# A gated graph layer followed by a normalised one: where the checks on newly loaded matrix rows stand at a change of batches

## The chip, the cores and the metric

The kernel runs on one core of one Trainium2 chip. The metric is the device time of one launch in microseconds (us). A core has five engines that run at the same time and each work through their own instructions in order: TensorE (PE in the profile; its weight loads are PEld), VectorE (DVE), ScalarE (ACT), GpSimd (POOL) and SyncE (SP), which here issues most of the transfers (DMAs) between the memory outside the core and its SBUF. TensorE writes into banks of PSUM, which VectorE and ScalarE read.

## What is computed

Sixteen graphs (batches) of 1024 nodes with 128 channels each go through two layers. `adj` holds a 1024x1024 matrix of zeros and ones for each batch.

```python
def gru_cell(m, h, w_ih, w_hh, b_ih, b_hh):
    xr, xz, xn = split(m @ w_ih.T + b_ih, 3)
    hr, hz, hn = split(h @ w_hh.T + b_hh, 3)
    r, z = sigmoid(xr + hr), sigmoid(xz + hz)
    n = tanh(xn + r * hn)
    return (1 - z) * n + z * h

# layer 0
h = maximum(layernorm(x), 0)
for i in range(4):
    m = einsum('bjn,bjd->bnd', adj, h @ weight[i])
    h = gru_cell(m, h, w_ih[i], w_hh[i], b_ih[i], b_hh[i])
x = x + h * nodemask
# layer 1
h = maximum(layernorm(x), 0)
for i in range(4):
    h = relu(einsum('bnm,bmc->bnc', adj, h @ W[i]) + b[i])
    h = gamma[i] * (h - mean(h)) * rsqrt(var(h) + eps) + beta[i]     # over batches and nodes
x = x + h
```

## The kernel before

The function `exact_path` computes both layers in a form that is exact only if the matrix entries can be held exactly in a shorter number format. Whether they can is read from their low 16 bits: every row tile of `adj` (128 rows by 1024 columns, float32) is looked through once, and the largest or summed low half goes into one column of the small tile `low`. If any is above zero, a general version runs afterwards. There are two ways to look through a row tile:

- `look` (line 606) is one VectorE reduction by maximum over the 1024 low halves (L610 in the profile);
- `glance` (line 580) is one ScalarE copy of the low halves with an accumulated sum (L586), for each row in its list. It writes its copy into a scratch tile called `junk`.

The first layer works on two streams of batches, A (`sa`: batches 0, 2, …) and B (`sb`: 1, 3, …). `half_step(one, two)` (line 1095) handles one iteration of each: stream `two` computes its gates, stream `one` its aggregation `adj.T @ h`. The calls alternate (`half_step(sa, sb)`, `half_step(sb, sa)`), each stream goes through four iterations for a batch (`self.i` from 0 to 3) and then takes the next one. The whole layer stands under a manual schedule: on every engine and queue the instructions run in the order in which the Python code emits them.

TensorE's part of a half step is `two.products(0)`, `two.products(1)` (the products for the gates, for columns 0 to 511 and 512 to 1023, called hf = 0 and 1) and then `one.agg_step(0)` and `one.agg_step(1)` (32 matmuls). Each gate has one PSUM bank, `g_r`, `g_z`, `g_hn`, `g_xn`, and both halves use the same four, so the products of hf = 1 can overwrite a bank only when what read it for hf = 0 is done. Around this, for each hf:

- `reset_gate`: sigmoid r on ScalarE (L1011), then two VectorE operations, L1012 (reads `g_hn`) and L1013 (reads `g_xn`);
- `candidate`: tanh on ScalarE (L1016);
- `less` (L1027 or L1029) and `mixed` (L1033, L1034) on VectorE; `update_gate`: sigmoid z on ScalarE (L1020, reads `g_z`);
- `high` (ScalarE) and `low` (VectorE, L942 or L926), for stream `one`: they split its features into two parts that the aggregation uses; `low(1)` is needed by `agg_step(1)`;
- at the end of `agg_step(1)`, two ScalarE copies of the result, `m` (L955), with which the next half step's products start.

Other work hangs on named places of a half step: `at(n, place, go)` (line 1059) enters a function for half step number n, and `due(place)` runs it. In order of emission the places are "ins", "start", "beside0", "mid", "beside1", "outs", "gap", "end". The norm of a batch to come is computed at "beside0" and "beside1", the sums of a finished batch at "gap".

The change of batches: when stream `two` is in its last iteration (`self.i == 3`) and has a batch to come, `fetch` (line 853) has SyncE load that batch's first four row tiles into four staging places (L572). Both streams use the same four places, A in one half step and B in the next. `first_four` (line 862) has GpSimd cast them into the row tiles that TensorE reads (L577). `last_four` (line 866), emitted behind z of hf = 1, emits four glances on ScalarE, one for each of rows 0 to 3, then the loads of rows 4 to 7 into the same four places, which must wait for the glances and casts of the rows before them, and their casts. Rows 4 to 7 are looked at in the following half step: for A by four looks at "start", so ahead of `reset_gate(0)` on VectorE, and for B by four glances at "gap". There are seven changes for each stream. In the half step after A's change comes B's, so B's first four loads wait for A's looks.

SyncE's queue in such a half step holds, in order: the incoming copies of a new batch's turned features ("ins", `pair_in`), the loads of rows 0 to 3, the outgoing copy of hf = 0, the loads of rows 4 to 7, the outgoing copies of hf = 1 and, at "end", of a turned input (`t_in`).

The second layer follows the first on the same core. It converts the stored matrix row by row and is not touched.

Of the kernel before, what the change touches and what calls it, by code (L numbers as in the profile page):

```python
# [341 lines left out]
def exact_path(  # L342
# [24 lines left out]
    NB = N // P  # L367
# [33 lines left out]
    def hw_tiles(b, name):  # L401
        return [keep.tile([P, N], F32R, tag=f"hw{b % 2}{s}", name=f"{name}_{s}") for s in range(2)]
# [130 lines left out]
    with ExitStack() as st:  # L533
# [36 lines left out]
        def stage_rows(b, stage, js):  # L570
            for j in js:
                nc.sync.dma_start(stage[j % 4], adj[b][j * P : (j + 1) * P, :])  # L572

        def round_rows(b, stage, js):
            ts = [gru_row(b, j) for j in js]
            for j, t in zip(js, ts):
                nc.gpsimd.tensor_copy(t, stage[j % 4])  # L577
            return ts

        def glance(b, stage, js):  # L580

            junk = work.tile([P, N], BF16, tag="junk", name=f"junk{b}_{js[0]}", bufs=1)
            for j in js:
                lows = stage[j % 4].bitcast(U16).rearrange("p (n t) -> p n t", t=2)[:, :, 0]
                k = b * NB + j
                nc.scalar.activation(junk, lows, AF.Copy, accum_out=low[:, k : k + 1])  # L586
# [19 lines left out]
        def look(b, row, j, part=0):  # L606

            lows = row.bitcast(U16).rearrange("p (n t) -> p n t", t=2)[:, :, 0]
            k = (b + part * B) * NB + j
            nc.vector.tensor_reduce(low[:, k : k + 1], lows, axis=AX.X, op=ALU.max)  # L610
# [7 lines left out]
        def transposes(batches):  # L618

            for b, rows in batches:  # L620
                adjT = turned_tile(f"adjT{b}")
                ahead = transpose_rows(b, rows[0], 0, adjT)
                for j in range(NB):
                    go = ahead
                    if j + 1 < NB:
                        ahead = transpose_rows(b, rows[j + 1], j + 1, adjT)
                    go()
                    yield j
                nc.gpsimd.dma_start(adjT_d[b].rearrange("k p n -> p k n"), adjT)
                yield NB  # L630
# [139 lines left out]
        class Stream:  # L770
# [95 lines left out]
            def last_four(self):  # L866
                if self.stage:
                    b, stage, self.stage = self.b + 2, self.stage, None
                    glance(b, stage, range(4))
                    stage_rows(b, stage, range(4, NB))  # L870
                    self.rows += round_rows(b, stage, range(4, NB))

                    def looks():
                        for j in range(4, NB):
                            look(b, stage[j % 4], j)

                    if self is sa:
                        at(clock[0] + 1, "start", looks)
                    else:
                        at(clock[0] + 1, "gap", lambda: glance(b, stage, range(4, NB)))  # L880

            def take(self):
                self.xt, self.y = self.next_x, self.next_y
# [173 lines left out]
        clock = [3]  # L1057

        def at(n, place, go):
            agenda.setdefault((n, place), []).append(go)  # L1060

        def due(place):
            for go in agenda.pop((clock[0], place), ()):
                go()
# [23 lines left out]
        def mids(two):  # L1088

            pace = small.tile([P, 1], F32, tag="pace", name=f"pace{clock[0]}")  # L1090
            nc.gpsimd.tensor_copy(pace, two.new[:, :1])
            feed.store()
            due("mid")

        def half_step(one, two, gated=None, halfway=None):

            feed.next_step()
            counts = (2, 1, 1)
            if one is sb and one.i == 0:
                feed.jobs = transposes([(s.b, s.rows) for s in (sa, sb)])  # L1100
                counts = (0, 0, 0)
            elif two is sb and two.i == 0:
                counts = (2, 2, 1)
            elif two is sa and two.i == 1 and two.across:
                counts = (3, 1, 1)
            due("ins")
            due("start")
            if one.i > 0:
                one.halves_back()
            else:  # L1110
                one.hw = hw_tiles(one.b, f"ghw{one.b}_0")
            two.fetch()
            feed.some(counts[0])
            two.products(0)
            two.reset_gate(0)
            due("beside0")
            two.candidate(0)
            two.less(0)
            one.high(0)
            two.update_gate(0)  # L1120
            one.low(0)
            two.mixed(0)
            two.half_away(0)
            two.first_four()
            if feed.full or (clock[0], "mid") in agenda:
                mids(two)
            one.high(1)
            feed.some(counts[1])
            two.products(1)
            two.reset_gate(1)  # L1130
            due("beside1")
            one.low(1)
            two.candidate(1)
            two.less(1)
            two.update_gate(1)
            two.last_four()
            two.mixed(1)
            two.half_away(1)
            due("outs")
            due("gap")  # L1140
            due("end")
            if gated:
                gated()
            one.agg_step(0)
            if halfway:
                halfway()
            feed.some(counts[2])
            one.agg_step(1)
            two.finish()
            clock[0] += 1  # L1150

        sa, sb = Stream(0), Stream(1)
        every = {getattr(mybir.EngineType, e) for e in ("PE", "DVE", "Activation", "Pool", "SP")}
        prep = st.enter_context(tc.tile_pool(name="prep", bufs=1))
        with tc.manual_schedule(engines=every):
# [20 lines left out]
            stage = keep.tile([P, NB, N], BF16, tag="adjT", name="stage", bufs=1).bitcast(F32)  # L1176
# [98 lines left out]
            first_step(sb, sa, lambda: turn_ih(prep, w_g, 2), lambda: ahead(2))  # L1275
            written[0] = False
            half_step(sa, sb, lambda: turn_ih(prep, w_g, 3), lambda: ahead(3))
            half_step(sb, sa)
            for s in range(3, B // 2 * L):
                half_step(sa, sb)  # L1280
                half_step(sb, sa)
# [301 lines left out]
```

## Time and profile before

| | |
|---|---|
| three runs | 1785.47, 1788.07, 1794.2 us; median 1788.07 |
| the profiled execution | 1789.26 us, its span 1787.5 |
| TensorE's granted clock | 0.999 |
| glances: count, one | 84; 1.06 us, and 0.19 for reading the sum |
| looks at staged rows: count, one | 36 (28 of them in the change of batches); 1.22 us |
| casts of staged rows on GpSimd: count, one | 112; 1.04 us median |
| loads of staged rows: count, size, issue to landing | 112; 512 KB; 3.5 / 5.7 / 7.9 us (least, median, most) |

All times of the profile belong to one execution. In a timeline a line has the start and the duration in us, the engine, the line of the kernel, what is done, and in brackets how long the engine had been idle and what ended it; merged instructions have a count. SPq is SyncE's queue: its lines are the issuing of transfers and not the transfers. A list of waits gives who waited for whom, the total in us, the number of times and the longest. A table of stretches gives the length, then each engine's busy time and number of instructions, TensorE's clock, and the share of time and the rate of the DMA engines.

### The profile page before, as it was taken

The page shows a single profiled execution, that of the slowest core. Times are in us where ns is not written, and L with a number is a line of the kernel's source. Part 1 is how long each engine was busy: PE and PEld are TensorE (multiplying, and loading weights), DVE is VectorE, ACT ScalarE, POOL GpSimd, SP SyncE. Part 2 cuts the span into 40 slices and gives each one's busy share as a digit, 9 for nine tenths or more (in the row PEclk, how much of TensorE's full clock was granted, in tenths as well). Part 3 has the DMA queues.
Part 4 walks back from the last instruction along what each step waited for, and adds up shares of the span by engine and source line. Part 5 has one row for each costly group of instructions (what it writes and reads, how often), then busy time and mean ns, then how long its engine had stood idle before and what let it go on. Part 6 is the DMA issues. An engine that isn't in the chain of part 4 may idle for free. (4 is left out here: it accounts for less than half of the span.)

```text
span 1787.5 us, 22335 instructions
## 1 busy us (share of the span) xinstructions
PE 1759.3 (98%) x6734; PEld 1191.7 (67%) x6734; DVE 1305.9 (73%) x2310; ACT 1107.6 (62%) x1713; POOL 379.3 (21%) x417
## 2 busy tenths in 40 slices
PE   9999999999999999999999999999999999999997
PEld 6565655565656565556555556577778888888886
DVE  7677877887887787887797787676666666666665
ACT  5356556556566556665655655476777767768765
POOL 4314323332331331422432333010100000000011
PEclk9999999999999999999999999999999999999999
DMA  7467657777676676776756768788766575767667
GB/s 259 135 175 262 189 163 272 179 208 241 204 200 213 223 212 197 245 202 202 260 169 186 265 174 227 256 287 311 271 228 241 207 253 201 245 224 245 238 217 268
DMA packets 363617, 400.16 MB, mean 224 GB/s; under 512 B 158188, under 2 KB 239888, under 8 KB 363488
## 3 DMA queue, kind: packets, MB, share of 16 engines
q1 hardware_dynamic: 342736, 323.59, 57.6%
q0 software_dynamic: 20224, 74.80, 11.3%
q8 instruction: 55, 0.90, 0.2%
q14 instruction: 74, 0.61, 0.1%
q10 hardware_dynamic: 528, 0.26, 0.0%
HBM read 267.47 MB, written 97.52 MB: 204 GB/s over the span
## 5 line engine op out<-in xcount | busy, mean ns | idle before, releaser
L524 PE MATMUL pm<-row,ghw 128*128 128x512 f32 x2048 | 503.6, 402 | 0.7 <-DVE ghw L926 0.6
L524 PEld LDWEIGHTS pm<-row,ghw 128*128 128x128 f32 x2048 | 383.8, 188 | 106.6 <-issue 29.2
L1016 ACT ACTIVATE r<-r,vecs 128x512 f32<-128x512 f32 x128 | 92.6, 723 | 255.0 <-DVE r L1013 253.1
L524 PE MATMUL pc_m<-wide,chw 128*128 128x512 f32 x1024 | 245.3, 395 | 0.0
L615 POOL CAST half<-row 128x1024 bf16<-128x1024 f32 x128 | 147.4, 1161 | 361.1 <-DMA adjT<-half 347.9
L524 PEld LDWEIGHTS pc_m<-wide,chw 128*128 128x128 f32 x1024 | 190.4, 188 | 41.9 <-issue 3.8
L524 PE MATMUL pc_g_r<-wide,chw 128*128 128x512 f32 x464 | 186.9, 403 | 0.3 <-ACT chw L501 0.3
L524 PE MATMUL pc_g_z<-wide,chw 128*128 128x512 f32 x464 | 181.0, 390 | 0.0
L577 POOL CAST row<-stage 128x1024 fp32r<-128x1024 f32 x112 | 128.6, 1156 | 243.7 <-DMA stage<-in_adj_dram 232.2
L1012 DVE SCALAR_TENSOR_TENSOR r<-g_hn,vecs,r 128x512 f32<-128x512 f32 x128 | 93.3, 729 | 117.9 <-ACT r L1011 66.9
L955 ACT COPY m<-pm 128x512 f32<-128x512 f32 x128 | 68.4, 585 | 163.5 <-PE pm L524 163.5
L1313 DVE CAST wide<-block 128x1024 fp32r<-128x1024 bf16 x160 | 109.9, 692 | 75.5 <-PE pc_m L524 48.3
L1313 DVE CAST wide<-packed 128x1024 fp32r<-128x1024 bf16 x160 | 110.1, 691 | 71.9 <-PE pc_g_z L524 53.5
L1311 ACT CAST wide<-packed 128x1024 fp32r<-128x1024 bf16 x96 | 100.6, 1048 | 58.5 <-PE pc_m L524 29.7
L993 PE MATMUL g_r<-m,w_mT 128*128 128x512 f32 x256 | 132.0, 597 | 3.4 <-ACT m L955 2.9
L1311 ACT CAST wide<-block 128x1024 fp32r<-128x1024 bf16 x96 | 100.7, 1049 | 53.9 <-PE pc_g_z L524 27.7
L993 PE MATMUL g_z<-m,w_mT 128*128 128x512 f32 x256 | 130.7, 592 | 0.0
L993 PE MATMUL g_xn<-m,w_mT 128*128 128x512 f32 x256 | 130.7, 592 | 0.0
L1361 DVE BATCH_NORM_STATS2 stats<-feat 128x6 f32<-128x512 f32 x128 | 84.1, 686 | 47.0 <-ACT feat L1360 45.9
L1029 DVE TENSOR_TENSOR h<-h,r 128x512 f32<-128x512 f32 x96 | 83.8, 872 | 41.9 <-ACT r L1016 41.8
L1033 DVE TENSOR_TENSOR h<-h,z 128x512 f32<-128x512 f32 x128 | 107.8, 842 | 6.8 <-ACT z L1020 0.2
L1011 ACT ACTIVATE r<-g_r,brz 128x512 f32<-128x512 f32 x128 | 87.9, 686 | 39.1 <-PE g_r L993 38.8
(186 smaller groups left out, 2830.5 us busy)
## 6 DMA issues: line engine op xcount, KB each, us to landing
block<-adjT_d SPq DMA_DIRECT2D x256, 256.0 KB, 4.7
packed<-adjT_d SPq DMA_DIRECT2D x256, 256.0 KB, 5.5
stage<-in_adj_dram SPq DMA_DIRECT2D x120, 512.0 KB, 5.7
adjT_d<-adjT POOLq DMA_DIRECT2D x16, 2048.0 KB, 7.7
cross_h<-t_h SPq DMA_DIRECT2D x92, 256.0 KB, 2.2
n_h<-cross_h SPq DMA_DIRECT2D x368, 64.0 KB, 2.0
xmid_d<-x POOLq DMA_DIRECT2D x16, 512.0 KB, 6.9
y<-ymid_d POOLq DMA_DIRECT2D x16, 512.0 KB, 5.4
```

The costliest lines, as they stand in the source:

```text
L524: nc.tensor.matmul(pm[hf], hw[s][:, j * P : (j + 1) * P], rows[j][:, hf * HALF : (hf + 1) * HALF], start=(j == 0 and s == 0), stop=(j == N ...
L577: nc.gpsimd.tensor_copy(t, stage[j % 4])
L615: nc.gpsimd.tensor_copy(t, row.bitcast(F32))
L993: nc.tensor.matmul(po, wT[:, i, g * C : (g + 1) * C], rhs, start=start, stop=stop)
L1011: nc.scalar.activation(r, pr, AF.Sigmoid, bias=brz[:, 3 * i : 3 * i + 1])
L1012: nc.vector.scalar_tensor_tensor(r, phn, b_hn(i), r, ALU.add, ALU.mult)
L1016: nc.scalar.activation(self.r, self.r, AF.Tanh, bias=b_in(self.i))
L1029: nc.vector.tensor_sub(ho, hin, self.r)
L1033: nc.vector.tensor_mul(ho, ho, self.z)
L1311: nc.scalar.copy(r, t)
L1313: nc.vector.tensor_copy(r, t)
L1361: nc.vector.bn_stats(stats[:, b * NH + hf, :], dst)
```

## The change

Only places in the order change. At both streams' changes the glances at rows 0 and 1 go ahead of `candidate(1)`, the tanh of hf = 1, behind sigmoid r (and behind what stands at "beside1"); those at rows 2 and 3 stay where they were, behind z. In the half step after A's change, the looks at rows 4 and 5 stay at "start" and those at rows 6 and 7 go to a new place "looks", behind `reset_gate(0)` and ahead of `less(0)` on VectorE. In the half step after B's, the glances at rows 4 and 5 go to "beside1", ahead of the tanh of hf = 1, and those at rows 6 and 7 stay at "gap".

```diff
             def last_four(self):
                 if self.stage:
                     b, stage, self.stage = self.b + 2, self.stage, None
-                    glance(b, stage, range(4))
+                    glance(b, stage, range(2, 4))
                     stage_rows(b, stage, range(4, NB))
                     self.rows += round_rows(b, stage, range(4, NB))
 
-                    def looks():
-                        for j in range(4, NB):
-                            look(b, stage[j % 4], j)
-
                     if self is sa:
-                        at(clock[0] + 1, "start", looks)
+                        for place, js in (("start", (4, 5)), ("looks", (6, 7))):
+                            at(clock[0] + 1, place, lambda js=js: [look(b, stage[j % 4], j) for j in js])
                     else:
-                        at(clock[0] + 1, "gap", lambda: glance(b, stage, range(4, NB)))
+                        for place, js in (("beside1", (4, 5)), ("gap", (6, 7))):
+                            at(clock[0] + 1, place, lambda js=js: glance(b, stage, js))
+
+            def first_glances(self):
+                if self.stage:
+                    glance(self.b + 2, self.stage, range(2))
...
             two.products(0)
             two.reset_gate(0)
             due("beside0")
+            due("looks")
             two.candidate(0)
             two.less(0)
             one.high(0)
...
             two.products(1)
             two.reset_gate(1)
             due("beside1")
+            two.first_glances()
             one.low(1)
             two.candidate(1)
             two.less(1)
```

## The prediction

> **What bounds the kernel now.** I read the page's first part first:
>
> ```profile
> PE 1759.3 (98%) x6734; PEld 1191.7 (67%) x6734; DVE 1305.9 (73%) x2310; ACT 1107.6 (62%) x1713; POOL 379.3 (21%) x417
> ```
>
> TensorE looks full, but matmul ends are modelled, so a short hold hides in it. I therefore took, from the timeline of TensorE, the start of the first hidden-state product (g_r<-h) of every half step of the first layer. They are numbered k = 0, 1, 2 … from 20.02 us. From k = 4 on, a half step takes 17.57 us unless it lies at a change of batches. Excess over 17.575 us:
>
> - k = 7, 15, 23, 31, 39, 47, 55 (stream B fetches): 1.49, 2.36, 2.09, 2.06, 0.75, 1.44, 2.38; sum 12.57
> - k = 8, 16 … 56: 0.30 to 0.37; sum 2.42
> - k = 9, 17 … 57: 0.01, 0.31, 0.11, 1.07, 0, 1.30, 1.03; sum 3.82
> - k = 34: 0.88; k = 6, 14 … 54 (stream A fetches) and all others: 0
>
> So the changes cost 19.7 us, 1.1% of the run; that is the most this change can win back. Stretches of k = 6, 7, 8:
>
> ```profile
> 133.38:150.96 17.58, 17.58 (x58) 10.57 (x57) 13.21 (x17) 14.92 (x28) 5.50 (x5) 1.00 0.61 207
> 150.96:170.03 19.07, 18.10 (x58) 10.38 (x56) 14.82 (x18) 9.91 (x17) 8.83 (x8) 1.00 0.85 296
> 170.03:187.91 17.88, 17.87 (x57) 10.49 (x56) 13.23 (x25) 10.98 (x21) 6.84 (x6) 1.00 0.67 197
> ```
>
> The second column is the length, then PE, PEld, DVE, ACT, POOL. No engine is full in k = 7; something is late. The timeline of k = 7 shows what:
>
> ```profile
> 146.75 3.87 SPq L572 DMA_DIRECT2D stage<-in_adj_dram  x4
> ...
> 150.33 1.22 DVE L610 TENSOR_REDUCE low<-stage 128x1 f32<-128x1024 uint16 x1
> ...
> 152.76 1.22 DVE L610 TENSOR_REDUCE low<-stage 128x1 f32<-128x1024 uint16 x1 [1.21 <-DMA stage<-in_adj_dram]
> ...
> 154.84 1.22 DVE L610 TENSOR_REDUCE low<-stage 128x1 f32<-128x1024 uint16 x1 [0.86 <-DMA stage<-in_adj_dram]
> ...
> 156.36 1.22 DVE L610 TENSOR_REDUCE low<-stage 128x1 f32<-128x1024 uint16 x1 [0.30 <-DMA stage<-in_adj_dram]
> 156.42 2.34 SPq L572 DMA_DIRECT2D stage<-in_adj_dram  x4
> ...
> 157.50 0.74 DVE L1012 SCALAR_TENSOR_TENSOR r<-g_hn,vecs,r 128x512 f32<-128x512 f32 x1
> 158.29 0.30 PEld L993 LDWEIGHTS g_hn<-h,w_hhT 128*128 128x128 f32 x2 [1.14 <-DVE r L1012]
> ...
> 160.94 0.30 PEld L993 LDWEIGHTS g_z<-h,w_hhT 128*128 128x128 f32 x2 [1.49 <-ACT z L1020]
> ```
>
> The four looks stand ahead of the first half's gates on VectorE and follow the rows as these land. The gate's first VectorE operation starts 6.54 us into the step; in k = 9, without looks, 2.85. TensorE may not overwrite the g_hn bank until it has read it, nor g_z until ScalarE's z, which is late by the same chain. The list of TensorE's waits names these two, and little else:
>
> ```profile
> PE g_z L993 <- ACT z L1020: 5.0, 8, 0.7
> PE g_hn L993 <- DVE r L1012: 4.6, 6, 1.2
> ```
>
> Why do the rows land late? They are sent (146.75) as the four glances behind z(1) finish:
>
> ```profile
> 145.53 1.05 ACT L586 ACTIVATE junk<-stage 128x1024 bf16<-128x1024 uint16 x1
> ```
>
> SyncE waited for glances in 56 cases, 79.0 us. In k = 8 the excess is ScalarE's: in k = 7 the glances end at 170.54, after the products (170.03), so the copies of m start 0.42 us late. In k = 9 it is VectorE's: the sums of the tail, started up to 17.2 us into k = 8, hold the gate.
>
> **What the Trainium skill says.** "TensorE: Matmul & The Clock Gate", Architectural detail, calls ScalarE and VectorE strict FIFO: a look or glance whose row hasn't landed holds all behind it. The trace agrees (the looks wait 20.0 us on rows in 24 cases; the gate stays behind them). "SBUF — State Buffer", Two separate sides, has VectorE's operations with two SBUF inputs lock a port pair with GpSimd: here the same 128x512 operation takes 0.69 us, and 1.25 to 1.52 beside a cast. "DMA: Bandwidth & Descriptors", Issuing engines are not separate DMA queues: all transfers share 16 engines; here a row lands after 3.6 us when sent nearly alone, 5.4 to 6.5 as the first of four.
>
> **The change part by part.** Nothing is added or removed: 84 glances and 36 looks stay. Times are from a half step's start.
>
> *Two glances ahead of A's tanh (k = 6, 14 …).* A pair costs 2.4 us of ScalarE (starts 1.18 apart: 145.53, 146.71). After sigmoid r(1) and the norm blocks ScalarE is free at +9.35; tanh waits for VectorE till +10.30 to +11.85. Rows 0 and 1 have landed by then (their casts start at +6.6 to +9.0 and some 1.2 later). So tanh starts at +11.85 everywhere: no loss, up to 1.5 late. VectorE's mixing then ends as in k = 14, about +15.6, and stream B's t_in transposes at +16.8. No TensorE write waits for this. Glances 2 and 3 end at +15.3 and not +16.9 to +17.8. Rows 4 and 5 are sent at about +10.7 and +11.8 instead of +12.7 to +15.5, rows 6 and 7 at +14.2 and +15.4. SyncE has only the second half's outgoing copies (t_out, t_in) behind them, not yet ready. Landing, at 3.6 to 5 us each: rows 4 and 5 at +14.3 and +16.4, rows 6 and 7 at +18.5 and +20.5, which is +0.9 and +2.9 in k = 7.
>
> *Two looks at the start, two behind the gates (k = 7, 15 …).* Looks 4, 5 run from -0.8 to +1.6, before the gate is ready (+2.85): cost nothing. The gate's pair ends at +4.6; looks 6, 7 add 2.44 us, to +7.05, covered by tanh up to +5.4, so less(0) starts 1.6 late (but at +8.9 to +9.8 before). From less(0) to the end of low(1) the trace has 5.4 to 6.1 us: +12.5 to +13.1. The second half of the aggregation needs it at 9.90 + 3.84 = +13.74. Margin 0.6 to 1.3. z(0) hangs on tanh, at +5.9: in time. I take 0.2 us left in each: gain 12.57 - 7 x 0.2 = 11.2. Bounds: all 12.6, or low(1) 1 us late.
>
> *B's first glances (k = 7).* SyncE sends rows 0, 1 behind eight copies: 4.9 to 5.8 us after the first t_in copy, so about +4.5, not +4.7 to +6.3. Rows 2, 3 wait for looks 6, 7: +5.9 and +7.1. At 5.4 to 6.5 us row 0 lands at +10 to +11, row 1 up to 1.2 later. Behind the waiting glances stand tanh(1), z(1), two glances and the m copies. From row 1: 1.18 + 0.63 + 0.57 + 2.56 = 4.9 us; m is due at +17.54, so row 1 may land as late as +12.6. It should make it by 0.4 to 1.6 us. Then k = 8 loses its 2.42.
>
> *B's later glances in pairs (k = 8).* Rows 4, 5 have landed by its start. ScalarE has 2.4 us between r(1) (ends +8.0) and tanh (+10.9 at best): hidden. The other pair stays, ending before +17.5.
>
> *Follow-up.* Rows sent earlier in k = 7 bring the casts of k = 8 forward, so that fewer of VectorE's operations meet one (each costs 0.7). I take 2.6 of the 3.82 in k = 9; bounds 0 and 3.8. The 0.88 of k = 34 I leave. Late next in every step is TensorE itself.
>
> **Sum.** 11.2 + 2.4 + 2.6 = 16.2 us. The profiled execution took 1789.26 (span 1787.5 and 1.8 around it): 1773.1. The median of the runs stands 1.2 lower. I say 1773. The second layer hangs on TensorE alone (its waits there: 0.3 us), so it passes the gain on.
>
> **Rivals.**
>
> *Half of it comes back.* The looks behind the gates, stretched by casts (0.7 us each on two or three of less, low and mixing), push low(1) to +14.7, 1 us late seven times, and VectorE's lateness keeps k = 9 as it is: 16.2 - 5.6 - 2.6 = 8.0, or 1781. For it: 0.6 us of margin. Against: casts of new rows start only at +10, when less and low(0) are past.
>
> *The limit is the landing.* Rows compete for the 16 DMA engines (85% busy in k = 7), so sending earlier doesn't land them earlier: looks 6, 7 wait for row 7 until +5.4 to +6.3 as now, less starts at +7.5, low(1) ends at +13.6 plus casts; B's glances give back the rest: 1787. For it: rows land 1.5 to 2.9 us apart now. Against: the queue has slack before, and row 4 landed in 3.6 us.
>
> *Slower.* B's first glances hold ScalarE before tanh(1), z(1) and the m copies. Each microsecond of row 1 past +12.6 is a microsecond of TensorE, seven times; from +14.9 all of 16.2 is used up, and at +16.3 it is 1799. For it: strict order, no cover. Against: it takes 10 us from sending to landing, and the longest of the 112 is 7.9.
>
> **How the numbers follow.** Forecast (1767 to 1779) 66%, half 16%, landing 9%, slower 9%. Noise and 0.5% (8.9 us, what a measurement can tell) put the border of faster at 1779: 0.68 of the forecast and half cases together; same 0.23; slower 0.09. Range: all of 19.7 gone is 1769, 1767 with the median's offset and scatter; up to the half case with the casts doubled, 1785. That leaves 2 in 10 out.
>
> **What would show it.** Steps 7, 15 … at 17.6 to 17.9, the gate on VectorE at +3 there; the waits of g_hn and g_z on TensorE gone; rows 4 sent 2 us earlier; steps 8 at 17.57 with the m copies unheld. Wrong: waits of tanh or glances on row landings in k = 7 beyond +12.6, or of pm on low(1).

## The result, and the profile after

The changed kernel takes 1819.28 us (median of 5 runs, 1817.71 to 1822.47), the kernel before in the same series 1789.79. The ratio is 1.016, with a 95% interval of 1.0147 to 1.0173: 1.6% slower, where 1773 and a range of 1767 to 1785 were forecast. The profiled execution took 1817.71 us with a span of 1815.9, so the span grew by 28.4.

The page's busy times show hardly anything:

```profile
PE 1766.9 (97%) x6734; PEld 1201.3 (66%) x6734; DVE 1285.2 (71%) x2310; ACT 1108.1 (61%) x1713; POOL 372.6 (21%) x417
```

TensorE has 7.6 us more busy time and the same instructions. The half steps, taken from start to start as for the prediction, say more (excess over 17.575 us, summed over the seven changes of batches):

| half steps | before | after |
|---|---|---|
| k = 7, 15 … 55 (B's change) | 12.57 | 46.15 |
| k = 8, 16 … 56 | 2.42 | 0 |
| k = 9, 17 … 57 | 3.82 | 0 |
| single ones (k = 20, 34, 59) | 0.88 | 2.2 |

In k = 7, 15 … the excess is now 5.7 to 8.0 us each. The sum of all rows rises by 28.7, close to the 28.4 of the span. TensorE's list of waits (who for whom, total in us, times, longest) has a new first line:

```profile
PE pm L524 <- DVE ghw L944: 32.0, 7, 5.0
...
PE g_z L995 <- ACT z L1022: 2.0, 2, 1.3
```

The wait of g_hn is gone, that of g_z is down from 8 cases to 2, as forecast, but seven times the aggregation waits for `low(0)` (now L944), 4.6 us on average. VectorE's list has the reason:

```profile
DVE low L610 <- DMA stage<-in_adj_dram: 51.5, 7, 7.8
```

Before, looks waited 20.0 us for rows in 24 cases, 0.8 each; now there are 7 waits of 7.4. The timeline of k = 7 of the changed kernel (it starts at 151.39; lines of the engines concerned) shows which row it is:

```profile
150.16 2.31 DVE L610 TENSOR_REDUCE low<-stage 128x1 f32<-128x1024 uint16 x2
...
152.85 1.04 POOL L577 CAST row<-stage 128x1024 fp32r<-128x1024 f32 x1 [2.05 <-DMA stage<-in_adj_dram]
...
154.24 0.75 DVE L1014 SCALAR_TENSOR_TENSOR r<-g_hn,vecs,r 128x512 f32<-128x512 f32 x1 [1.77 <-PE g_hn L995]
...
155.10 0.69 DVE L1015 TENSOR_TENSOR r<-g_xn,r 128x512 f32<-128x512 f32 x1
155.15 2.35 SPq L572 DMA_DIRECT2D stage<-in_adj_dram  x4
155.19 1.04 POOL L577 CAST row<-stage 128x1024 fp32r<-128x1024 f32 x1 [1.29 <-DMA stage<-in_adj_dram]
...
160.72 1.04 POOL L577 CAST row<-stage 128x1024 fp32r<-128x1024 f32 x1 [4.49 <-DMA stage<-in_adj_dram]
...
161.94 1.04 POOL L577 CAST row<-stage 128x1024 fp32r<-128x1024 f32 x1 [0.18 <-PE g_z L995]
...
163.08 2.44 DVE L610 TENSOR_REDUCE low<-stage 128x1 f32<-128x1024 uint16 x2 [7.29 <-DMA stage<-in_adj_dram]
...
163.18 1.04 POOL L577 CAST row<-stage 128x1024 fp32r<-128x1024 f32 x1 [0.19 <-DMA stage<-in_adj_dram]
...
165.43 0.68 DVE L1031 TENSOR_TENSOR h<-h,r 128x512 f32<-128x512 f32 x1
166.03 0.68 DVE L944 TENSOR_TENSOR ghw<-y_in,ghw 128x512 fp32r<-128x512 f32 x1
...
166.77 8.51 PE L524 MATMUL pm<-row,ghw 128*128 128x512 f32 x30 [4.44 <-DVE ghw L944]
```

GpSimd casts A's rows 6 and 7 at 152.85 and 155.19, so both have landed by the time the gate's pair ends on VectorE (155.79). The looks start at 163.08, within 0.1 us of the cast of the third of the four rows sent at 155.15. That is row 2 of stream B's new batch. Behind them stand `less(0)` and `low(0)`, and the aggregation waits for `low(0)`.

The places of the code explain it. The place "looks" is emitted behind `fetch`. By then `fetch` has emitted B's loads of rows 0 to 3 into the same four staging places. A look at place 2 that is emitted behind a load into place 2 reads what that load brings. In the compiled program the four looks of such a half step wait for the completion of these loads (queue numbers):

```
look 4: DMAHW0    look 5: DMAHW1    look 6: DMAHW5    look 7: DMAHW6
A's loads of rows 4 to 7: DMAHW0 to DMAHW3    B's loads of rows 0 to 3: DMAHW3 to DMAHW6
B's loads of rows 0 and 1 wait for VectorE; those of rows 2 and 3 do not
```

B's load of row 0 also waits until A's row 7 has landed, because the two loads use the same queue, DMAHW3. This wait, and not the one for A's looks, is the last to end in the kernel before: in all seven changes that load goes out 0.07 to 0.09 us after row 7 has landed (k = 7: 156.34 and 156.42), while the look at row 7 still runs until 157.58. In the changed kernel it is the last in five of the seven.

So the changed kernel looks at B's rows 2 and 3 (which its glances read as well) and not at A's rows 6 and 7. That part of the computation is left out in it.

### The profile page after: what moved, and what is told of

It reads as the page before. It is cut to its first block, busy times and chain, and to the rows that moved or that the text cites. A ratio compares the mean times of both kernels' runs of the same rounds, so it can differ in the third digit from the quotient of the medians.

```text
span 1815.9 us, 22328 instructions
## 1 busy us (share of the span) xinstructions
PE 1766.9 (97%) x6734; PEld 1201.3 (66%) x6734; DVE 1285.2 (71%) x2310; ACT 1108.1 (61%) x1713; POOL 372.6 (21%) x417
## 5 line engine op out<-in xcount | busy, mean ns | idle before, releaser
L524 PE MATMUL pm<-row,ghw 128*128 128x512 f32 x2048 | 518.2, 410 | 33.0 <-DVE ghw L944 32.0
L524 PEld LDWEIGHTS pm<-row,ghw 128*128 128x128 f32 x2048 | 392.0, 192 | 145.4 <-DVE ghw L944 35.1
L577 POOL CAST row<-stage 128x1024 fp32r<-128x1024 f32 x112 | 123.7, 1109 | 263.4 <-DMA stage<-in_adj_dram 254.2
L1036 DVE TENSOR_TENSOR h<-h,r 128x512 f32<-128x512 f32 x128 | 102.3, 800 | 4.3
```

What stands on the lines that cost most here:

```text
L524: nc.tensor.matmul(pm[hf], hw[s][:, j * P : (j + 1) * P], rows[j][:, hf * HALF : (hf + 1) * HALF], start=(j == 0 and s == 0), stop=(j == N ...
L1036: self.last_dve = nc.vector.tensor_add(ho, ho, self.r)
```

## The experiments

The theory: the late looks wait for B's loads because they are emitted behind them ("order"). Its rivals: rows 6 and 7 land late because the loads compete ("landing"), or the first glances hold ScalarE ("glances"). Each ratio below is to the kernel before in the same series (medians 1790.44 for the first four, 1790.55 for the last three), with its 95% interval.

**Fetch behind the looks.** One line of the changed kernel moves; SyncE's order stays.

```diff
-            two.fetch()
             feed.some(counts[0])
             two.products(0)
             two.reset_gate(0)
             due("beside0")
             due("looks")
+            two.fetch()
```

> Order theory: the looks at places 6 and 7 are emitted behind fetch, so what they read is B's new rows 2 and 3 in the same staging places, and they wait for those loads. With fetch emitted behind the looks (nothing else stands between on SyncE's queue) they read A's rows 6 and 7, landed by +3 us of the half step; the steps of B's change go from 23 to 25.5 us back to 17.6 to 17.9, and the time to 1771 to 1777. Landing theory: rows 6 and 7 themselves land late because the loads compete for the DMA engines; then the looks wait for about 7 us as now and the time stays at 1815 to 1825. Glance theory: the first glances of B hold ScalarE; then the time stays above 1800 too.

Measured: 1770.7 us, ratio 0.9887 (0.9867 to 0.9908). All half steps of the changes (k = 6 to 9 and so on) now take 17.57 us. The timeline of its k = 7 (start 150.98), in the same lines:

```profile
149.76 2.31 DVE L610 TENSOR_REDUCE low<-stage 128x1 f32<-128x1024 uint16 x2
...
153.83 0.75 DVE L1014 SCALAR_TENSOR_TENSOR r<-g_hn,vecs,r 128x512 f32<-128x512 f32 x1 [1.77 <-PE g_hn L995]
...
154.69 0.69 DVE L1015 TENSOR_TENSOR r<-g_xn,r 128x512 f32<-128x512 f32 x1
...
154.90 3.12 SPq L572 DMA_DIRECT2D stage<-in_adj_dram  x4
...
155.29 2.33 DVE L610 TENSOR_REDUCE low<-stage 128x1 f32<-128x1024 uint16 x2
...
157.55 0.68 DVE L1031 TENSOR_TENSOR h<-h,r 128x512 f32<-128x512 f32 x1
```

The late looks follow the gate with no wait, and `less(0)` starts 6.57 us into the step. No look waits for a landing in this kernel, in any of the seven changes. The landing theory falls: the same rows, no wait. So does the glance theory: the glances stand where they stood.

**Four looks at the start.** The changed kernel with its moves of glances, and the looks as before.

```diff
-                        for place, js in (("start", (4, 5)), ("looks", (6, 7))):
+                        for place, js in (("start", (4, 5, 6, 7)),):
```

> All four looks at the start of the half step again, the three moves of glances kept. Order theory: nothing waits for B's rows any more; the rows land 2 to 3 us earlier than before the change, so the fourth look ends at about +5 us and the gate follows, in time for the g_hn bank at +6.9: 1771 to 1779. Landing theory: the looks follow the rows as before the change, steps of B's change at 18.3 to 20: 1783 to 1790. Glance theory: 1800 or more.

Measured: 1771.32 us, ratio 0.9888 (0.9867 to 0.9909). In k = 7 its looks end at +4.6 us and the gate's first operation starts there, before g_hn is needed; no excess is left in the steps of the change. The looks need no place behind the gates once the rows come earlier.

**The move of two looks alone**, in the kernel before, in the place where the change has it (so again the late looks read B's rows 2 and 3):

```diff
-                    def looks():
-                        for j in range(4, NB):
-                            look(b, stage[j % 4], j)
-
                     if self is sa:
-                        at(clock[0] + 1, "start", looks)
+                        for place, js in (("start", (4, 5)), ("looks", (6, 7))):
+                            at(clock[0] + 1, place, lambda js=js: [look(b, stage[j % 4], j) for j in js])
...
             due("beside0")
+            due("looks")
```

> The kernel before, with the move of two looks alone. Order theory: B's rows 2 and 3 are sent about 1.5 us later than in the changed kernel and land at about +13 to +14, so the steps of B's change take 25 to 28 us: 1825 to 1845, slower than with the whole change. Landing theory: the looks behind the gates wait for rows 6 and 7, which land at +5 to +6: 1780 to 1792. Glance theory: no first glance stands ahead of a tanh, so 1780 to 1790.

Measured: 1839.13 us, ratio 1.0265 (1.0243 to 1.0287). B's loads go out at 157.61 here, 6.0 us into k = 7 (3.8 in the changed kernel), and the late looks start at +13.9. Two lines of its timeline (k = 7 starts at 151.60):

```profile
165.47 2.45 DVE L610 TENSOR_REDUCE low<-stage 128x1 f32<-128x1024 uint16 x2 [9.47 <-DMA stage<-in_adj_dram]
...
169.17 9.77 PE L524 MATMUL pm<-row,ghw 128*128 128x512 f32 x30 [6.64 <-DVE ghw L939]
```

A's row 7 lands 2.3 us later than in the changed kernel (+5.9 and +3.7), B's rows 2.2 us later, and TensorE waits 2.2 us longer. The order theory's number holds (62.1 us of excess in the seven steps, which take 25.0 to 27.6 us).

**Late looks left out.**

```diff
-                        for place, js in (("start", (4, 5)), ("looks", (6, 7))):
+                        for place, js in (("start", (4, 5)),):
```

> The changed kernel without the two looks behind the gates (rows 6 and 7 of A's batches are not looked at), 14 reductions fewer. Order and landing theory: 1770 to 1776, since VectorE waits for no load behind the gates. Glance theory: 1800 or more, since the glances are where they were.

Measured: 1770.07 us, ratio 0.9882 (0.9861 to 0.9903). Without these 14 looks the loss is gone, and with them in the right order (1770.7) it is gone as well: in the right order they cost nothing that can be measured.

The three parts of the change, each alone and in the right order:

**First glances alone**: the diff of the four looks at the start, and B's four later glances together again.

```diff
-                        for place, js in (("beside1", (4, 5)), ("gap", (6, 7))):
-                            at(clock[0] + 1, place, lambda js=js: glance(b, stage, js))
+                        at(clock[0] + 1, "gap", lambda: glance(b, stage, range(4, NB)))
```

> The kernel before with the first glances ahead of the tanh, nothing else: four looks at the start, B's four later glances together at the gap. If the gain of the right order comes from rows sent earlier, it is all here, 1771 to 1776; B's four later glances may end just past +17.5 us and hold the m copies by up to 0.4 us seven times. If it comes from the looks behind the gates, this stays at 1782 to 1790.

Measured: 1770.43 us, ratio 0.989 (0.9875 to 0.9906). The whole gain is here, 0.6 us below the range expected. B's four glances at the gap held the m copies in one of the seven changes (0.52 us of excess in k = 25, none in the other six).

**Looks alone, fetch behind them**: the diffs of the looks alone and of fetch together.

> The kernel before with two looks behind the gates and fetch behind them, glances as before. If the looks ahead of the gate were the hold, the 12.6 us of the steps of B's change go and the 2.4 us of the steps after them (late m copies behind four glances) stay: 1775 to 1781. If rows sent earlier are what counts, look 7 still waits until about +6 us and the second half's low is late: 1782 to 1790.

Measured: 1776.55 us, ratio 0.9926 (0.9913 to 0.9939). The steps k = 7, 15 … have 0.6 us of excess left of 12.6, and the steps after them 3.1: 1.6, 0.8 and 0.7 in three of the seven, where the four glances end behind the products. The steps k = 9, 17 … keep 1.4. The first line of TensorE's waits in this kernel is the one that was expected to stay, products waiting for m copies:

```profile
PE g_r L990 <- ACT m L952: 3.5, 6, 1.3
```

So each move is a cure for the looks ahead of the gate; the glances cure the late m copies too.

**Later pairs alone**, in the kernel before:

```diff
-                        at(clock[0] + 1, "gap", lambda: glance(b, stage, range(4, NB)))
+                        for place, js in (("beside1", (4, 5)), ("gap", (6, 7))):
+                            at(clock[0] + 1, place, lambda js=js: glance(b, stage, js))
```

> The kernel before with B's later glances in two pairs, nothing else. These lie in the step after B's change, whose excess comes from the glances of the step before, and the next step's excess is VectorE's: 1786 to 1792, no change. If B's four glances at the gap were what holds the next step, 1784 or less.

Measured: 1787.69 us, ratio 0.9985 (0.9974 to 0.9996). That is 2.9 us faster, with an interval of 0.7 to 4.7 us: clear of zero, but no change by the prediction's bound of 0.5%. The profiled execution is one of the slower of this kernel's runs (1791.4): its steps k = 7, 15 … have 17.1 us of excess, 4.5 more than in the profile of the kernel before, for a reason that is not known, the steps after them 3.8, and the steps k = 9, 17 … none.

The last of these is the work of the pairs, and it shows what had held k = 9, 17 … in the kernel before. The list of waits there has a third line that the prediction passes over, and the timeline around the start of k = 49 (903.72, excess 1.30) shows its cause:

```profile
PE g_r L993 <- ACT m L955: 2.9, 4, 1.0
```

```profile
904.07 1.06 ACT L586 ACTIVATE junk<-stage 128x1024 bf16<-128x1024 uint16 x1
...
905.13 1.05 ACT L955 COPY m<-pm 128x512 f32<-128x512 f32 x2
...
905.74 1.13 PE L993 MATMUL g_r<-m,w_mT 128*128 128x512 f32 x2 [1.00 <-ACT m L955]
```

The last of B's four glances at the gap starts 0.35 us into the new step, so the m copies start at +1.4 and TensorE waits for them. Over the seven changes these copies start at -0.03, 0.45, 0.22, 1.21, -0.03, 1.40 and 1.16, and the excess is 0, 0.31, 0.11, 1.07, 0, 1.30 and 1.03. With the pairs alone, k = 9 starts at 188.52:

```profile
188.49 1.07 ACT L956 COPY m<-pm 128x512 f32<-128x512 f32 x2 [0.94 <-PE pm L524]
...
192.91 0.73 DVE L1013 SCALAR_TENSOR_TENSOR r<-g_hn,vecs,r 128x512 f32<-128x512 f32 x1
```

ScalarE is idle before the copies, and the step has no excess although VectorE's gate starts as late as +4.4. All five kernels with the later pairs have no excess in any of these steps; the four without them keep 0.5 to 3.9 us. The expectation of 1784 or less for this case was itself too low: with 3.8 us at stake the time could fall to about 1787.

## Why the prediction was wrong, point by point

- **What bounds the kernel** held: the excess at the changes was there to be had. It is 18.8 us and not 19.7, since the prediction's sum takes in the 0.88 of k = 34, which is no change. With the order right it is gone; 1770.7 us is 19.7 below that series' 1790.44, with an interval of 16 to 24.
- **The step that failed** is in "Two looks at the start, two behind the gates" and in its counterpart under B's first glances, "Rows 2, 3 wait for looks 6, 7". I took the late looks to read A's rows 6 and 7, landed at +0.9 and +2.9 (their casts start at +1.5 and +3.8), and B's loads to wait for them. Both are the wrong way round in the emitted order: B's loads go first and the looks wait for them. The looks ended at +14.1 and not at +7.05. I had placed the looks by what they were named for on VectorE and not followed the staging place that they share with SyncE's loads, although `fetch` stands a few lines above in `half_step`. That the change does not do what it says was to be considered as a rival, and I had none of that kind.
- **The price of that step**: `low(0)` is needed by the third of the 32 aggregation matmuls, which starts at +10.76 with the order mended. In k = 7 it came at +15.3, and over the seven changes TensorE went on at +14.7 to +15.9. My slower rival had the right sign and a wrong place: it held ScalarE behind B's first glances. In the changed kernel these start at +9.3 and +10.8, earlier than estimated, and hold nothing. The late landing it feared did not come either: row 1 was there by +10.8 in k = 7, within the limit of +12.6.
- **A's first glances** held: the tanh of k = 6 starts at +11.48 (+11.85 was said), the loads of rows 4 to 7 begin at +10.47 (+10.7), and no TensorE write waited.
- **B's first glances** held in effect: the steps k = 8 lost their 2.42. The glances of k = 7 end 1.3 us before the m copies in the changed kernel, whose step is 6 us longer, and 2.4 us before them with the order mended. The start of B's loads was put down to the copies ahead of them; in five of the seven changes it hangs on the landing of A's row 7, and it came at +2.9 to +4.0 where +4.5 was said. Their first row takes 5.3 to 6.3 us to land in the kernel before (5.4 to 6.5 was said) and 5.2 to 5.9 in the changed one.
- **The later pairs** were said to cost and gain nothing. With the first glances in place that is so (1771.32 with the pairs, 1770.43 without, each in its own series). Alone they take away all 3.8 us of k = 9, 17 …, which the prediction had put down to VectorE.
- **The follow-up** was right in sign, by luck: the wait that it named was not the one. It had the late gate on VectorE hold these steps, and earlier casts cure it; what held TensorE was the m copies behind B's glances. Earlier rows do help, by a longer way: in the first glances alone, 13 of VectorE's two-input operations in k = 8, 16 … take over 0.9 us instead of 22, and 3.3 of the 3.8 us go without the pairs (2.6 was said). That fewer slowed operations let the glances begin earlier is a reading of the order on the engines; no run changes the casts alone.
- **The sum** of 16.2 came out too low for the mended order: the 1.4 us that I had left in the steps k = 7, 15 … went too, and the 1.2 us that the follow-up lacked. The rest lies within the interval. The 1773 is the profiled execution's figure; with the 1.2 us by which the median stands lower it is 1771.9.
- **The landing and the half-back rivals** fall: with the order mended, rows 6 and 7 make no look wait, and `low(1)` comes in time.

## What to carry to other kernels

A read that is moved past the issue of a load into its own buffer changes what it reads and what it waits for, while every count of instructions stays as it was. Before a moved instruction gets a price, list, for every buffer it touches, the writes between its old and its new place on all queues. Where a reader must go later on its engine, move the refill behind it in the code as well: here that cost nothing that can be measured, and the refilling queue's order stayed the same. And before a step's lateness is put down to an engine that is late, read which wait of the bound engine ends last there: VectorE was late in k = 9, 17 …, but TensorE waited for ScalarE's copies.

## What the runs showed of the hardware

A long wait of TensorE costs more than its length. In k = 7 of the changed kernel the excess is 6.16 us and the wait 4.44. The table of stretches of that half step (length, busy times with counts, then the granted clock, the DMA share and GB/s) shows the rest:

```profile
151.39:162.30 10.91, 10.91 (x27) 4.75 (x25) 2.52 (x3) 6.00 (x11) 3.48 (x4) 1.00 1.01 320
162.30:166.77 4.47, 0.03 (x2) 0.00 (x1) 3.69 (x5) 1.03 (x2) 2.76 (x3) 0.96 0.26 106
166.77:170.00 3.23, 3.23 (x8) 2.60 (x9) 3.06 (x5) 0.00 (x0) 0.00 (x0) 0.53 0.11 44
170.00:175.12 5.12, 5.12 (x24) 4.20 (x23) 3.60 (x6) 3.52 (x7) 1.75 (x2) 1.00 0.91 322
```

In the 3.23 us after the wait the clock is at 0.53 of full speed and 8 matmuls start; at the pace of the last stretch (24 in 5.12 us) 15 would. From start to start a matmul takes 0.43 us just behind the wait and 0.23 later. Over the seven changes the waits of 3.8 to 5.0 us sum to 32.0 and the excess to 46.15: 14.1 us, nearly a third, lie outside the waits, 1.7 to 3.1 each. About 0.2 us in each of these is no loss of the clock: the profile models the end of the matmul before the wait, and counted from when the next one should have started, 1.5 to 3.0 us are left.

The extra does not grow with the wait. In the move of two looks alone the seven waits are 5.1 to 8.1 us long and 1.8 to 3.0 us lie outside each. The slow stretch behind a wait lasts 3.1 to 6.1 us in all fourteen cases, and about half of it is lost.

One wait of the later pairs alone is shorter, 2.83 us for the g_hn bank in its k = 15, and has the same consequence:

```profile
305.00:308.00 3.00, 3.00 (x5) 1.28 (x4) 2.55 (x4) 2.51 (x5) 1.15 (x1) 0.52 0.97 373
```

The next shorter one of that kernel, 1.48 us in k = 31, leaves the clock at 1.00.

The Trainium skill, "TensorE: Matmul & The Clock Gate", What's actually happening, has the array at half rate after an idle window of about 3.4 us and at full rate after a busy window of the same length. The half rate agrees. The lengths agree only roughly: a wait of 2.83 us was enough here, and the slow stretch took up to 6.1 us. No wait between 1.5 and 2.8 us was measured in the half steps, so these runs do not show where the limit lies. The prediction's prices of a late TensorE ("a microsecond of TensorE" for each of row 1) leave this out. In the kernel before, whose waits in these steps are 1.2 us at most, the clock of k = 7 is 1.00, so its profile shows nothing of it.
